# A hybrid network of four layers on one core: convolution by blocks, decays in two parts, output pieces between the scan's steps, and row updates in layer 2

## The chip, the cores and the metric

The kernel is one program on one core of a Trainium2 chip. The core's engines run side by side, each with its own queue of instructions in a fixed order: TensorE (PE, with PEld for its weight loads), VectorE (DVE), ScalarE (ACT), GpSimd (POOL) and SyncE (SP, which here only issues transfers). They wait for each other through semaphores. The metric is the device time of one execution in microseconds (us).

## The reference

The input is x, 4 images of 256 channels by 32x32 places, so 1024 tokens an image and 4096 in all. Everything is float32. What bears on the change is layer 0 (a Mamba-2 block with channel attention) and layer 1:

```python
# layer 0
u = layernorm(tokens(x))                              # eps 1e-5, norm_g, norm_b
z, xBC, dt = split(u @ in_w.T)                        # 256, 512, 4
dt = softplus(dt + dt_bias)
xBC = silu(conv4(xBC) + conv_b)                       # causal, each channel by itself, 4 taps
xs, Bm, Cm = split(xBC)                               # 256 (4 heads of 64), 128, 128
state = state * exp(dt * A) + (dt * x_t) outer B_t    # a scan over the 1024 tokens
y = state @ C_t + Dp * xs
y = y * silu(z);  y = y * rsqrt(mean(y * y) + eps) * rms_w
out = y @ out_w.T
attn = sigmoid(relu(mean_over_tokens(out) @ se1_w.T + se1_b) @ se2_w.T + se2_b)
x = x + out * attn
# layer 1
g, theta, phi = (w @ x + b for each)                  # one number a token
y = theta * sum_over_image(phi * g) / 1024
x = x + (w_w * y - mean) * rsqrt(var + eps) * bn_gamma + bn_beta   # mean, var by channel
```

Layer 2 is attention over each image's 1024 tokens and then a feed-forward layer of 8 experts, of which each token takes two; layer 3 is attention in another form, and an LSTM of 1024 steps.

## The kernel before

A scheduler of the language orders each engine's queue when the kernel is built: instructions go by their place in the program, but one that is ready earlier may move ahead. Only the ends of the attention, the plan of the experts and the LSTM have their order written out by hand. Tiles come from pools with a fixed number of buffers; a new tile waits until an old one is released.

The residual stream lies in SBUF as `rows`, 32 tiles of 128 tokens by 256 channels.

- `_project` walks over 8 blocks of 512 tokens: a block of x is loaded and turned (p_x, L241; ACT copies it to `rows`, L244, and DVE keeps three sums a token for layer 1, of_x, L245), moments by DVE (L133, L134), rstd by POOL (L146, L147), scaling by DVE (L153), turned back (L162, u by ACT, L257), and projected: p_z gives silu(z) (ACT, L273) and dtr (DVE, L274), p_w the 512 channels of xBC (L278, copied by ACT, L281). After every second block `convolve` runs over a whole image of 1024 tokens: for each of 4 groups of 128 channels a scaling by ACT (L288), three taps by DVE (L293), each onto the same `acc`, and a Silu by ACT (L296).
- `_decays` comes once, after all of it: softplus and its products for all 32 tiles in DVE, with Exp and Ln on ACT, and three matmuls (L350) whose Exp gives `head`, `total` and `tail`.
- `_scan` takes an image in 8 steps of 128 tokens: transposes and C by B (ptr, L370, L371), decays within the tile (au by ACT, L381; pd, L383; Exp to m_h, L385; times gm by DVE, L386), products with x (xdt, y, xw by POOL, L389, L395, L398; py, L392), the state's share (pst, L401, L406; DVE, L403, L404, L408, L409), then zs by DVE (L412) and its sum of squares by ACT (L414).
- `_out` does an image's output in one go: rstd by POOL (L426, L427), for each tile a diagonal matrix of rstd by DVE (L434) that PE turns y with (L438; yT by ACT, L442, which also sums up `part`), the channel attention (L447 to L467), the weights times attention (L469), six accumulating products by DVE (L473) for the three columns that layer 1 wants, and eight products (L481), added to `rows` by DVE (L484), with the three columns copied by ACT (L485). The order in the program is scan 0, scan 1, out 0, scan 2, out 1, scan 3, out 2, out 3.
- `_layer1` makes one row and one number a token (L505 to L549), adds bn_beta to `rows` by POOL in 8 pieces (L552) and row times y by DVE in 32 (L554).
- `_layer2_attention` multiplies wq by wk to m_qk (L602 to L612), and its `front` normalises, turns and projects an image. Then scores (p_s, L739), maxima (L744), Exp (L748), transposes (L760) and products (L773) go token tile by token tile.

PSUM has 8 banks: p_x 2, p_z 2 and p_w 4 in the projection; ptr 2, p_o 2, pst 2, pd 1 and py 1 in the scan. The weights of layer 0 come in one load (`w_l0`, 1092 KB, on ACT's queue); `wide` brings five rows of 256 to all partitions.

Of the kernel before, what the change touches and what calls it, by code (L numbers as in the profile page):

```python
# [19 lines left out]
B = 4  # L20
# [51 lines left out]
NW = {"w_l0": 260 + 512 + 256 + 64, "w_l2": 768 + 8, "w_l3": 768, "w_u": 768, "w_v": 768}  # L72
# [92 lines left out]
def _layer0_and_1(s):  # L165

    nc, tc = s.nc, s.tc
    off = DCONV - 1  # L170
    with ExitStack() as ctx:
        keep = ctx.enter_context(tc.tile_pool(name="l0_keep", bufs=1))
        w = keep.tile([P, C, NW["w_l0"]], F32, name="w_l0")
        nc.scalar.dma_start(w, s.d["w_l0"].rearrange("(k p) n -> p k n", p=P))
        se2 = keep.tile([NSE, D], F32, name="se2")
        nc.scalar.dma_start(se2, s.d["w_se2"])
        wide = keep.tile([P, 5, D], F32, name="wide")
        nc.scalar.dma_start(
            wide.rearrange("p i d -> p (i d)"), s.d["wide"].to_broadcast([P, 5 * D])
        )  # L180
        v = SimpleNamespace(
            w_zdt=w[:, :, :ZDT], w_xbc=w[:, :, ZDT : ZDT + 512], w_out=w[:, :, 772:1028],
            w_se1=w[:, :, 1028:1092], se2=se2, se2_b=wide[:, 0, :], beta=wide[:, 1, :],
            three=wide[:, 2:, :],
# [3 lines left out]
            xbc=[keep.tile([P, NXBC, off + L], F32, name=f"xbc{b}") for b in range(B)],  # L188
            zs=[keep.tile([P, TPI, D], F32, name=f"zs{b}") for b in range(B)],
            dtr=keep.tile([P, NT, NH], F32, name="dtr"),  # L190
            ss=keep.tile([P, NT], F32, name="ss"),
        )
        for x in v.xbc:
            nc.gpsimd.memset(x[:, :, :off], 0.0)
        for k in range(C):
            nc.vector.tensor_scalar_mul(
                v.w_out[:, k, :], v.w_out[:, k, :], s.col["rms_w"][:, k : k + 1]
            )
        _project(s, v)
        v.dt, v.decay, v.total, v.tail = _decays(s, keep, v.dtr)  # L200
        with ExitStack() as body:
            pools = SimpleNamespace(
                scan=body.enter_context(tc.tile_pool(name="ssm", bufs=2)),
                out=body.enter_context(tc.tile_pool(name="out", bufs=2)),
                ps=body.enter_context(tc.tile_pool(name="ssm_ps", bufs=2, space=PSUM)),
            )
            for b in range(B):
                _scan(s, v, pools, b)
                if b > 0:
                    _out(s, v, pools, b - 1)  # L210
            _out(s, v, pools, B - 1)
        _layer1(s, v)


def _project(s, v):
# [4 lines left out]
    with ExitStack() as ctx:  # L220
        one = ctx.enter_context(tc.tile_pool(name="proj_one", bufs=1))
        pool = ctx.enter_context(tc.tile_pool(name="proj", bufs=2))
        ps = ctx.enter_context(tc.tile_pool(name="proj_ps", bufs=3, space=PSUM))

        turner = one.tile([P, C, 3 + P], F32, name="turner")
        for k in range(C):
            nc.vector.tensor_copy(turner[:, k, 3:], s.ident)
            for j, name in enumerate(("theta_w", "phi_w", "g_w")):
                nc.vector.tensor_copy(turner[:, k, j : j + 1], s.col[name][:, k : k + 1])
        held = {}  # L230

        def load(i):
# [4 lines left out]
            for j in range(TPB):  # L237
                n = i * TPB + j
                p = ps.tile([P, C, 3 + P], F32, name="p_x", bufs=2)
# [6 lines left out]
            at = slice(i * TPB, (i + 1) * TPB)  # L246
            held[i] = _moments(s, pool, lambda j: s.rows[:, i * TPB + j, :], TPB)
            un = pool.tile([P, TPB, D], F32, name="un")
            _normalise(s, pool, un, s.rows[:, at, :], held[i])
            held[i] = un  # L250
# [12 lines left out]
        def project(i):  # L263
            u = held.pop(i)
            b, t0 = divmod(i * W, L)
            for j in range(TPB):
                n = t0 // P + j
                p = ps.tile([P, ZDT], F32, name="p_z", bufs=2)
# [4 lines left out]
                nc.scalar.activation(v.zs[b][:, n, :], p[:, :D], AF.Silu)  # L273
                nc.vector.tensor_add(v.dtr[:, b * TPI + n, :], p[:, D:], s.row["dt_bias"])  # L274
            for m in range(NXBC):
# [5 lines left out]
                nc.scalar.copy(v.xbc[b][:, m, off + t0 : off + t0 + W], p)  # L281

        def convolve(b):
            for m in range(NXBC):
                x = v.xbc[b][:, m, :]
                acc = pool.tile([P, L], F32, name="acc")
# [5 lines left out]
                for j in range(off):  # L292
                    nc.vector.scalar_tensor_tensor(  # L293
                        acc, x[:, j : j + L], tap[:, j : j + 1], acc, ALU.mult, ALU.add
                    )
# [5 lines left out]
        for i in range(NBLK):  # L301
# [5 lines left out]
            if i % BPI == BPI - 1:  # L307
                convolve(i // BPI)


def _decays(s, keep, dtr):

    nc, tc = s.nc, s.tc
    shape = [P, NT, NH]
    dt = keep.tile(shape, F32, name="dt")
    a = keep.tile(shape, F32, name="a")
    head = keep.tile(shape, F32, name="head")
    total = keep.tile(shape, F32, name="total")  # L320
    tail = keep.tile(shape, F32, name="tail")
    with ExitStack() as ctx:
        pool = ctx.enter_context(tc.tile_pool(name="dec", bufs=1))
        ps = ctx.enter_context(tc.tile_pool(name="dec_ps", bufs=3, space=PSUM))

        e = pool.tile(shape, F32, name="e")
        nc.vector.scalar_tensor_tensor(e, dtr, -1.0, dtr, ALU.mult, ALU.max)
        nc.scalar.activation(e, e, AF.Exp, scale=-1.0)
        e1 = pool.tile(shape, F32, name="e1")
        nc.vector.tensor_scalar_add(e1, e, 1.0)  # L330
        num = pool.tile(shape, F32, name="num")
        nc.scalar.activation(num, e1, AF.Ln)
        none = pool.tile(shape, F32, name="none")
        nc.vector.tensor_single_scalar(none, e1, 1.0, ALU.is_equal)
        nc.vector.tensor_add(num, num, none)
        den = pool.tile(shape, F32, name="den")
        nc.vector.scalar_tensor_tensor(den, e1, -1.0, none, ALU.add, ALU.add)
        nc.vector.reciprocal(den, den)
        nc.vector.tensor_mul(num, num, den)
        nc.vector.tensor_mul(num, num, e)  # L340
        nc.vector.scalar_tensor_tensor(dt, dtr, 0.0, num, ALU.max, ALU.add)

        na = pool.tile([P, NH], F32, name="na")
        nc.scalar.activation(na, s.row["A_log"], AF.Exp)
        nc.vector.scalar_tensor_tensor(a, dt, -1.0, _bc(na, 1, NT), ALU.mult, ALU.mult)

        flat = a.rearrange("p n h -> p (n h)")
        for mat, dst in ((s.upper, head), (s.ones, total), (s.lower, tail)):
            p = ps.tile([P, NT * NH], F32, name="p")
            nc.tensor.matmul(p, mat, flat, start=True, stop=True)  # L350
            nc.scalar.activation(dst.rearrange("p n h -> p (n h)"), p, AF.Exp)
        nc.vector.tensor_mul(tail, tail, dt)
    return dt, (a, head), total, tail


def _scan(s, v, pools, b):


    nc, pool, ps = s.nc, pools.scan, pools.ps
    (a, head), xbc, zs = v.decay, v.xbc[b], v.zs[b]  # L360
    off = DCONV - 1
    state = pool.tile([P, NH, HD], F32, name="state")
    for c in range(TPI):
# [5 lines left out]
        for m in range(3):  # L369
            nc.tensor.transpose(ptr[:, m, :], xbc[:, m, t], s.ident)  # L370
# [1297 lines left out]
```

## Time and profile before

| | us |
|---|---|
| median of 4 runs | 3480.41 (3478.54 to 3484.51) |
| the profiled execution | 3479.1 |
| its span in the profile | 3477.4 |
| PE busy | 3118.7 (90%) |
| DVE busy | 1842.3 (53%) |
| ACT busy | 1091.1 (31%) |
| POOL busy | 535.1 (15%) |
| first pd matmul of the scan (L383) | 152.95 |
| last zs of the scan (L412) | 300.24 |
| layer 1's row ready (L549) | 347.9 |
| first scores of layer 2 (L739) | 384.34 |
| last scores of layer 2 | 690.2 |

The span is the time between the first and the last instruction that the profiler recorded. "Busy" is time in which the engine had an instruction at work; PE's ends are modelled. In the lists of instructions a row has its start, its length, the engine, the line, the operation and tiles, and in brackets how long the engine stood idle before it and what ended that. The chain of waits is followed back from the last instruction: at each step to what released it. Times in the text are from the start of the span.

### The profile page before, as it was taken

Reading aid. Unit: us, or ns where it says so; the run is one execution under the profiler, and the core shown is the slowest. Engines: PE = TensorE matmul, PEld = TensorE weight load, DVE = VectorE, ACT = ScalarE, POOL = GpSimd, SP = SyncE. Lnnn points to the kernel's source line nnn. Section 1 sums busy time; section 2 is a strip of 40 time slices with the busy share of each in tenths; the row PEclk is TensorE's granted clock in tenths of the full one; section 3 lists DMA queues with packets and bytes.
Section 4 is the critical chain, followed back from the end, with each engine's and each line's share of the span. In section 5 each row is a group of like instructions: output and inputs, shape, how many; then the busy total and the mean of one; then the engine's idle time right before and its main releaser. Section 6 shows DMA issues by size and latency. Waiting matters only on the chain.

```text
span 3477.4 us, 143620 instructions
## 1 busy us (share of the span) xinstructions
PE 3118.7 (90%) x63578; PEld 2506.6 (72%) x63578; DVE 1842.3 (53%) x8172; ACT 1091.1 (31%) x4347; POOL 535.1 (15%) x752
## 2 busy tenths in 40 slices
PE   8797899969999979898998998998998998998887
PEld 5465566758888866777777777777777777777776
DVE  5686555541111133565655655655655665665555
ACT  5663222222222222233333332332332332332222
POOL 1153000024444420000100100100100100100000
PEclk9898899979999999999999999999999999999999
DMA  2000000046666630000000000000000000000000
GB/s 81 1 1 19 1 25 26 30 160 191 193 193 192 202 102 1 3 4 4 10 4 4 10 4 4 10 4 4 10 4 4 10 4 4 10 4 6 8 4 10
DMA packets 46003, 135.51 MB, mean 39 GB/s; under 512 B 4864, under 2 KB 34880, under 8 KB 40768
## 3 DMA queue, kind: packets, MB, share of 16 engines
q0 software_dynamic: 19008, 99.32, 9.3%
q1 hardware_dynamic: 24496, 21.27, 1.9%
q8 instruction: 499, 8.18, 1.0%
q10 hardware_dynamic: 1872, 5.68, 0.5%
q14 instruction: 128, 1.05, 0.1%
HBM read 103.95 MB, written 22.32 MB: 36 GB/s over the span
## 4 chain that ended last, share of the span: by engine, by line
PE 54%; DVE 26%; ACT 11%; issue 5%; POOL 1%; DMA 1%; ACTq 0%; DVEq 0%; POOLq 0%; SPq 0%
PE pre L1500 15%; DVE col L1511 11%; PE ph L1111 7%; PE po L1121 7%; PE pre L1462 6%; ACT tri L1514 5%; DVE scan L1523 5%; DVE hs L1534 4%; PE p_a L1420 3%; PE p_d L773 3%; PE p_s L739 3%; DVE acc L293 1%; PE p_o L481 1%; PE p_d L1214 1%; PE p_w L760 1%
## 5 line engine op out<-in xcount | busy, mean ns | idle before, releaser
L1500 PE MATMUL pre<-w_v,hs 128*4 128x64 f32 x49104 | 873.7, 219 | 210.2 <-DVE hs L1534 199.5
L1500 PEld LDWEIGHTS pre<-w_v,hs 128*4 128x4 f32 x49104 | 685.1, 87 | 397.4 <-DVE hs L1534 396.9
L1462 PE MATMUL pre<-xg,pick 128*128 128x64 f32 x6144 | 904.8, 284 | 0.0
L1462 PEld LDWEIGHTS pre<-xg,pick 128*128 128x128 f32 x6144 | 764.5, 191 | 117.8 <-issue 0.8
L1511 DVE STREAM_TRANSPOSE col<-pre 128x64 f32<-128x64 f32 x2048 | 485.0, 250 | 304.1 <-PE pre L1500 286.1
L1514 ACT ACTIVATE tri<-col 128x16 f32<-128x16 f32 x1024 | 229.4, 224 | 1180.8 <-DVE col L1511 1180.8
L1523 DVE TENSOR_TENSOR_SCAN scan<-tri 128x24 f32<-128x24 f32 x1024 | 216.4, 211 | 361.4 <-ACT tri L1514 361.4
L1428 POOL TENSOR_TENSOR xg<-xg,gate_bias 128x192 f32<-128x192 f32 x128 | 75.5, 590 | 1593.0 <-ACT xg L1427 1593.0
L1111 PE MATMUL ph<-xT,wt 128*128 128x256 f32 x1152 | 257.2, 382 | 0.4 <-ACT hT L1114 0.4
L1121 PE MATMUL po<-wt,hT 128*128 128x256 f32 x1152 | 254.6, 379 | 0.0
L1114 ACT ACTIVATE hT<-ph,wt 128x256 f32<-128x256 f32 x288 | 136.2, 473 | 369.6 <-PE ph L1111 369.5
L1111 PEld LDWEIGHTS ph<-xT,wt 128*128 128x128 f32 x1152 | 208.8, 191 | 42.8 <-ACT hT L1114 4.2
L1121 PEld LDWEIGHTS po<-wt,hT 128*128 128x128 f32 x1152 | 216.6, 190 | 27.6
L1532 DVE STREAM_TRANSPOSE gate<-row 128x64 f32<-128x64 f32 x1024 | 227.8, 222 | 0.6
L1521 ACT ACTIVATE row<-pre 128x64 f32<-128x64 f32 x1024 | 209.8, 205 | 0.5
L1539 DVE SCALAR_TENSOR_TENSOR tri<-hs,scan 128x8 f32<-128x8 f32 x1023 | 181.3, 177 | 36.2 <-DVE hs L1534 1.7
L1085 DVE COPY xT<-p_x 128x512 f32<-128x512 f32 x36 | 24.9, 692 | 228.5 <-PE p_x L1081 228.5
L1135 POOL DMA_INDIRECT acc<-y,rows x72 | 114.9, 1596 | 187.7 <-issue 86.7
L1133 DVE TENSOR_TENSOR y<-po,wt 128x256 f32<-128x256 f32 x72 | 30.6, 425 | 204.9 <-PE po L1121 204.9
L1420 PE MATMUL p_a<-w_u,u 128*32 128x192 f32 x1792 | 119.3, 338 | 0.0
L773 PE MATMUL p_d<-v,prT 128*128 128x256 f32 x512 | 117.6, 380 | 0.4 <-DVE v L658 0.4
L739 PE MATMUL p_s<-u,q 128*128 128x512 f32 x256 | 116.3, 596 | 0.0
(2376 smaller groups left out, 3248.1 us busy)
## 6 DMA issues: line engine op xcount, KB each, us to landing
xn<-xn SPq DMA_DIRECT2D x8, 516.0 KB, 3.5
x<-in_x_dram SPq DMA_DIRECT2D x16, 256.0 KB, 3.2
rows<-acc SPq DMA_DIRECT2D x8, 512.0 KB, 7.1
out_dram<-part SPq DMA_DIRECT2D x64, 64.0 KB, 1.7
acc<-rows SPq DMA_DIRECT2D x7, 512.0 KB, 2.9
r<-xn,rows POOLq DMA_INDIRECT x72, 3.3
acc<-y,rows POOLq DMA_INDIRECT x72, 3.9
w_l<-in_w_l_dram ACTq DMA_DIRECT2D x1, 1092.0 KB, 9.8
```

The lines of the kernel that those rows point to most:

```text
L739: nc.tensor.matmul(p[:, h, :], v.q[:, k, bass.ts(j, P)], v.u[:, k, bass.ts(h, W)], start=k == 0, stop=k == C - 1,)
L773: nc.tensor.matmul(p, prT[:, n, :], images[g // TPI].v[:, n, :], start=n == 0, stop=n == TPI - 1)
L1111: nc.tensor.matmul(ph, w1[:, k, bass.ts(m, P)], xT[:, k, :], start=k == 0, stop=k == C - 1)
L1121: nc.tensor.matmul(po, hT[:, m, bass.ts(j, P)], w2[:, m, :], start=m == 0, stop=m == NHC - 1,)
L1420: nc.tensor.matmul(p[32 * j : 32 * (j + 1), :], u3[i * SG // P][:, k, bass.ts(i % (P // SG), 32)], w_u[:, k, j * Q : (j + 1) * Q], start=k ...
L1462: nc.tensor.matmul(p, pick[:, r].rearrange("p j r -> p (j r)"), xg[i][:, v], start=True, stop=t == 0,)
L1500: nc.tensor.matmul(p[32 * j : 32 * j + B, :], hs[:, t - 1, k * B : (k + 1) * B], w_v[:, k, j * Q + v.start : j * Q + v.stop], start=False, ...
L1511: nc.vector.transpose(col[:, g * C : (g + 1) * C, :].rearrange("p n r -> p (n r)"), pre[t % 2][g])
L1514: nc.scalar.activation(z[:, 2:50].rearrange("p (g q) -> p g q", g=2)[:, :, ::3].rearrange("p g (k b) -> p (g k) b", k=C), col[:, :, :B], A ...
L1521: nc.scalar.activation(row, pre[t % 2][2], AF.Tanh)
L1523: nc.vector.tensor_tensor_scan(scan, z[:, 0 : 3 * S], z[:, 26 : 26 + 3 * S], 0.0, ALU.mult, ALU.add)
L1532: nc.vector.transpose(gate.rearrange("p n r -> p (n r)"), row)
```

## The change

It touches layers 0 and 1 and the beginning of layer 2.

- **Convolution by blocks.** `xbc` holds each block of 512 tokens by itself with its own three columns in front; POOL copies a block's last three columns there for the next. Scaling, taps and Silu follow each p_w directly, over 512 tokens.
- **Decays in two parts.** Image 0's eight tiles after block 1, in the middle of the projection; the other 24 after step 1 of the scan.
- **Output pieces among the scan's steps.** `_out` is cut into `_turned` (two tiles), `_attended` and `_product` (one tile). `_scan` keeps a list of pieces and takes two after each step; what is left comes after the last.
- **Channel attention by small products.** The bias of se2 becomes a row of its weights. tanh is taken once as a row and once as a column; the factors 0.5 go into the weights. The three columns come from four matmuls of out_w's transpose with `a3` instead of six DVE products. out_w is transposed at the start (four transposes).
- **Moves.** m_qk (`_keys`) is made ahead of the last image's products, from a w_l2 that is loaded at the projection's end into the place of the input weights. bn_beta is added by POOL to each block of `rows` in the projection. The 32 row updates go into layer 2's `norm`, four before the moments of each block. The load of layer 0's weights is cut in two, with beta's between them.

```diff
-        _project(s, v)
-        v.dt, v.decay, v.total, v.tail = _decays(s, keep, v.dtr)
...
+            nc.scalar.dma_start(w, s.d["w_l0"][:, :NIN].rearrange("(k p) n -> p k n", p=P))
+            nc.scalar.dma_start(v.beta, s.d["bn_beta"].to_broadcast([P, D]))
+            nc.scalar.dma_start(w, s.d["w_l0"][:, NIN:].rearrange("(k p) n -> p k n", p=P))
+            _project(s, v, keep)
+        nc.scalar.dma_start(s.w_l2, s.d["w_l2"].rearrange("(k p) n -> p k n", p=P))
...
+                nc.tensor.transpose(p[:, bass.ts(m, P)], v.w_out[:, m, bass.ts(k, P)], s.ident)
+            nc.scalar.copy(v.w_outT[:, k, :], p[:, :D])
...
+            nc.gpsimd.tensor_add(mine, mine, _bc(v.beta, 1, TPB))
...
-                nc.scalar.copy(v.xbc[b][:, m, off + t0 : off + t0 + W], p)
-        def convolve(b):
-            for m in range(NXBC):
-                x = v.xbc[b][:, m, :]
-                acc = pool.tile([P, L], F32, name="acc")
+                x = v.xbc[b][:, m, half, :]
+                nc.scalar.copy(x[:, off:], p)
+                if half + 1 < BPI:
+                    nc.gpsimd.tensor_copy(v.xbc[b][:, m, half + 1, :off], x[:, W:])
+                acc = v.acc.tile([P, W], F32, name="acc")
...
-            if i % BPI == BPI - 1:
-                convolve(i // BPI)
+            if i == BPI - 1:
+                _decays(s, v, pool, lambda: ps.tile([P, ZDT], F32, name="p_z"), 0, TPI)
...
+def _scan(s, v, pools):
+    aside = []
+    for b in range(B):
+        yT = pools.out.tile([P, C, L], F32, name="yT", bufs=2)
+        part = pools.out.tile([P, C, TPI // 2], F32, name="part", bufs=2)
+        state = pools.scan.tile([P, NH, HD], F32, name="state")
+        for c in range(TPI):
+            _scan_tile(s, v, pools, b, c, state)
+            if b == 0 and c == 1:
+                _decays(s, v, pools.scan, lambda: _small(pools, P, W), TPI, NT)
+            for _ in range(2):
+                if aside:
+                    aside.pop(0)()
+            if c % 2:
+                aside.append(
+                    lambda b=b, c=c, yT=yT, part=part: _turned(s, v, pools, b, c - 1, yT, part)
+                )
+        w = []
+        aside.append(lambda w=w, part=part: w.append(_attended(s, v, pools, part)))
+        if b == B - 1:
+            aside.append(lambda: _keys(s, pools))
+        for c in range(TPI):
+            aside.append(lambda b=b, c=c, yT=yT, w=w: _product(s, v, pools, b, c, yT, w[0]))
+    while aside:
+        aside.pop(0)()
...
+def _turned(s, v, pools, b, c, yT, part):
+    rstd = pool.tile([P, 2], F32, name="rstd", bufs=3)
+    nc.gpsimd.tensor_scalar(rstd, v.ss[:, n : n + 2], 1.0 / D, EPS, ALU.mult, ALU.add)
+    nc.gpsimd.tensor_tensor(rstd, rstd, s.power[:, :2], ALU.pow)
+    for j in range(2):
+        nc.vector.tensor_scalar_mul(diag[:, j, :], s.ident, rstd[:, j : j + 1])
...
-    nc.vector.tensor_add(att, p, v.se2_b)
-    nc.scalar.activation(att, att, AF.Tanh, scale=0.5)
-    nc.vector.tensor_scalar(att, att, 0.5, 0.5, ALU.mult, ALU.add)
+    nc.scalar.activation(att, p, AF.Tanh, scale=0.5)
+            p[:, k : k + 1], v.se2[:, bass.ts(k, P)], hdn[:, 0:1], start=True, stop=True
+    nc.scalar.activation(att_c, p, AF.Tanh, scale=0.5)
...
-            nc.vector.scalar_tensor_tensor(
-                junk, w[:, k, :D], 1.0, v.three[:, j, :], ALU.mult, ALU.mult,
-                accum_out=w[:, k, D + j : D + j + 1],
-            )
+    nc.vector.scalar_tensor_tensor(a3, _bc(att_c, 2, 3), 1.0, v.three, ALU.add, ALU.mult)
+                p[:, bass.ts(m, 3)], v.w_outT[:, k, bass.ts(m, P)], a3[:, k, :],
+    nc.vector.tensor_copy(w[:, :, D:], p.rearrange("p (k j) -> p k j", k=C))
...
-        for i in range(NBLK):
-            mine = s.rows[:, i * TPB : (i + 1) * TPB, :]
-            nc.gpsimd.tensor_add(mine, mine, _bc(v.beta, 1, TPB))
-        for n in range(NT):
-            nc.vector.scalar_tensor_tensor(
-                s.rows[:, n, :], row, y[:, n : n + 1], s.rows[:, n, :], ALU.mult, ALU.add
-            )
...
             def norm(i):
                 n = b * TPI + i * TPB
+                for j in range(n, n + TPB):
+                    nc.vector.scalar_tensor_tensor(
+                        s.rows[:, j, :], s.l1_row, s.l1_y[:, j : j + 1], s.rows[:, j, :],
+                        ALU.mult, ALU.add,
+                    )
...
-    s.wpool = ctx.enter_context(tc.tile_pool(name="weights", bufs=2))
+    s.wpool = ctx.enter_context(tc.tile_pool(name="weights", bufs=1))
```

## The prediction

> **What bounds the kernel now.** I read the busy table and the slices first, then busy time by stage, then the chain of waits up to 420 us, then the timeline of the places that the chain names. In program order one core does layers 0 and 1 (to 348 us), layer 2's attention (to about 720), the experts, layer 3 and the LSTM. After layer 2's first steps the order of every engine is the same in both kernels, so only the first 390 us can change, and what they gain or lose reaches the end, since what follows is a serial chain.
>
> ```profile
> 28.00:130.00 102.00, 95.30 (x367) 58.90 (x365) 68.97 (x153) 70.21 (x119) 6.26 (x10) 1.00 0.04 11
> 130.00:153.00 23.00, 2.79 (x12) 2.53 (x13) 14.73 (x21) 14.39 (x24) 0.00 (x0) 0.58 0.00 0
> 153.00:213.00 60.00, 57.28 (x316) 42.06 (x315) 51.62 (x121) 44.64 (x134) 37.51 (x54) 0.96 0.01 1
> 213.00:300.00 87.00, 78.80 (x461) 61.61 (x460) 74.60 (x189) 47.71 (x156) 43.01 (x53) 1.00 0.00 1
> 300.00:338.00 38.00, 26.82 (x124) 20.18 (x124) 16.77 (x61) 7.92 (x31) 9.20 (x7) 0.82 0.00 0
> 338.00:361.00 23.00, 7.86 (x26) 6.12 (x26) 18.37 (x51) 0.91 (x3) 4.21 (x11) 0.66 0.19 69
> 361.00:384.00 23.00, 18.50 (x63) 11.63 (x64) 15.56 (x57) 3.92 (x6) 5.03 (x8) 0.82 0.00 0
> ```
>
> The columns are the stretch, its length, busy time of PE, PEld, DVE, ACT and POOL, PE's clock, and DMA. PE is full while it projects (28 to 130) and scans (153 to 300). In 130 to 153 it stands nearly idle, and from 300 to 384 it is partly idle. The chain says why:
>
> ```profile
> 134.99 4.88 DVE acc L293 x4
> 139.90 1.30 DVE acc L293
> 142.40 1.28 ACT L344
> 144.12 1.28 ACT L332
> 149.29 1.28 ACT L351
> 153.16 1.71 PE pd L383 x2
> ...
> 307.83 9.35 PE p_o L481 x32
> 328.20 9.38 PE p_o L481 x32
> 347.96 12.76 DVE rows L554 x32
> 384.50 6.87 PE p_s L739 x16
> ```
>
> Between projection and scan stand the last image's convolution and the decays. After the scan stand the output pieces of images 2 and 3, one after the other, layer 1's scalars, 32 row updates, and layer 2's first normalisations.
>
> **From projection to scan.** The mark is the scan's first pd matmul, at 153.16 now. (a) At the start PE has four transposes of w_out behind the first tile's products. They wait for a load that is now third instead of part of the first. The one load lands at 11.57 now and PE resumes at 12.33. Bounds: no delay, and the landing of today's third load of weights, "wide", issued at 6.86 and 7.5 on its way, 14.4, so 2.8 later; I take 1.5. (b) The convolution's 48 taps on DVE (1024 wide) become 96 of 512. Twelve in a row take 14.94, so 1.245 each; half is 0.62, and a 128x512 product (L386) takes 0.69. I take 0.66: 63.4 instead of 59.8. They start with block 0's first p_w (26.3, plus copy 0.58, scaling 0.66 and 1.5) at 29, no longer at 45.4. (c) The eight adds of beta (POOL L552, 2.35 each) now run in the projection. The timeline shows what they do to DVE:
>
> ```profile
> 280.61 2.37 POOL L552 TENSOR_TENSOR rows<-rows,wide 128x1024 f32<-128x1024 f32 x1 [1.58 <-DVE rows L484]
> 281.33 1.93 DVE L408 TENSOR_TENSOR state<-state,total 128x256 f32<-128x256 f32 x1
> ...
> 338.10 2.34 POOL L552 TENSOR_TENSOR rows<-rows,wide 128x1024 f32<-128x1024 f32 x1 [1.35 <-DVE rows L484]
> 338.25 2.31 DVE L505 TENSOR_TENSOR all<-all,of_y 128x96 f32<-128x96 f32 x1 [0.23 <-ACT of_y L485]
> ```
>
> L408 with both inputs in SBUF takes 0.41 elsewhere. It ends only when POOL does, while L484, which reads PSUM, keeps its 0.42 beside the same add. The taps read two SBUF tensors, and in DVE's order taps follow the scaling that each add waits for, from block 2 on: six adds by about 2.1 is 12.6; the bounds are 0 and 14.1.
>
> The Trainium skill (SBUF — State Buffer, "Who interferes with whom") says that a DVE instruction with two SBUF inputs contends with a GpSimd instruction that reads SBUF, the later one waiting in full. No row here shows a tap beside an add; by that rule all six meet, and without it this term is nought and the forecast 12.6 us lower.
>
> (d) DVE from 29 on: taps 63.4, locks 12.6, statistics and scaling of five more blocks (20 tiles by 0.9, from L133, L134, L153, L245 when they follow closely) 18, waits for rstd 5 by 1.24 (L153 idled 9.9 before eight), 30 dtr adds 2.4, the first decays 2: 105, so 134 without other idling. ACT gets six more table loads (1.28 each, 7.7) around the first decays, and DVE is 68% busy here now, so I add 6: 140. PE needs 26 for two blocks (32 passes of L278 by 0.43, 32 of L270 by 0.22, 32 of L241 and 16 of L162 by 0.11) and gets 29.4 today (L288 begins at 44.13, 73.57 and 103.01 in the chain), so it is not the later one. The decays' 9.4 us in series are gone. First pd at 140 instead of 153: 13 gained, between 3 (DVE 88% filled) and 22 (half the locks, no idling). Block-edge copies on POOL are three columns wide, cost under 0.2, and stand behind nothing that DVE waits for.
>
> **The scan.** L412 starts at 160.1 for step 1 and 213.1 for step 16: 3.53 us a step. The next sixteen, with the output pieces of images 0 and 1 in big lumps, take 87.1, so a lump costs (87.1 - 56.5)/2 = 15.3. First pd to last L412 (300.2) is 147. Afterwards three lumps lie inside and three of the four turnings of the last image: 7 + 32 by 3.53 + 3 by 15.3 + 2.9 (three quarters of L438's 3.89) = 169. Off it come: six accumulating products per image with the two passes on att (2.08 + 0.33 + 0.2, less 0.2 for the small ones), 3 by 2.4 = 7; the locks by the adds (L408 at 2.36, 1.91, 1.93 instead of 0.42: 4.9 in two lumps, 7.4 in three); and 3 for spreading. That last is bounded by 0 and by the lump's PE time, 12.5 (32 passes by 0.112, 32 by 0.22, two small products): 8.4 for three. On come 3 for the later decays: three table loads, 3.85, among ACT's work of about 3.0 in a step of 3.53. POOL changes little: 15 pairs of 0.2 + 0.71 (128x2, as L541) in place of three of 1.85 and four adds. Sum 154: 7 lost, between 4 gained and 18 lost. PE's own work in it is 32 by 3.2 (five passes for ptr and eight for py by 0.11, two for pd by 0.43, four for pst by 0.22) plus 3 by 12.5 plus 3, 143, so it fits.
>
> **After the scan.** From last L412 to layer 1's sum being done (340.59) is 40.3. Left are one turning of two tiles (sq 0.6, rstd 0.9, diag 0.4, PE 0.9, ACT 0.9, hand-overs: 5.4), attention 5.6 (6.4 now, from 321.82 to 328.20, less L465 and L467, plus the tiny products), the eight products 9.4 and the copy 0.2. The keys come in here: in PE's order the eight passes of wq by wk and four tiny ones stand ahead of the products and pass two PSUM buffers that ACT empties. Now they run at 348 to 353.6 under the row updates and cost nothing; with that cover gone, 3. The add lock on L505 goes (2.31 to 0.25). Sum 24: 16 gained, between 13 and 19.
>
> **Into layer 2.** From the row at 347.96 to the first scores at 384.34 is 36.4. Four updates (0.4 each) now precede the first statistics, and twelve more stand in DVE's order ahead of the scores. DVE idles 7.4 of the 23 us to 384 and can take some in. The gain is at least 12.8 - 6.4 = 6.4 and at most 12.8 - 1.6 = 11.2; I take 9. The last 16 updates stand around the first score maxima, where DVE waits 39.3 us over the stage for p_s: hidden; without that cover they cost 6.4. The load of w_l3 stands on ACT's queue ahead of layer 2's first copy of u, as it does now ahead of m_qk's; it waits there for DVE and POOL work that the copy comes after anyway. Its issue takes 0.5, and its 5.9 in flight are hidden until 1285 us, its first use. The load of w_l2 moves from 340.6 up to the end of the projection, behind the last product out of w_in, whose place it takes; ACT's last copy of p_w, three entries ahead in its queue, waits for the same product, and its landing (4.3) has the whole scan for cover.
>
> **Sum.** -13 + 7 - 16 - 9 = -31 on a span of 3477.4, in an execution of 3479.1 (1.7 lie around the span), 1.3 under the median of 3480.4. I forecast 3449.
>
> **Rivals.** (A) DVE becomes the bound of the projection: the taps idle as DVE does today, first pd comes at 153 or later. For it: the locks, the rstd waits, the table loads. Against: taps are spread, and 29.4 us per two blocks today holds a burst of 15. Gain 0 + 9 + 16 - 7 = 18 or less; about 3462. (B) The locks mostly miss (the adds fall beside statistics), and the scan goes at PE's rate, 145: 20 + 2 + 17 + 10 = 49; 3431. For it: PE was 95% busy from 153 to 213. Against: ACT and DVE have about 3 us a step as well. (C) Slower: the turnings block PE's queue. Each of the 15 puts four passes behind zs, sq, POOL's rstd pair and diag, 3.0 us of chain; POOL's pair stands in its queue behind later steps' xdt, y and xw (0.61 each), and a PE that waits holds the next step's matmuls. Fully exposed, 45; it decides from 2.1 each (31/15) and would give 3494. Against: in PE's order each turning stands one or two steps after its last zs. (D) The time comes back later, say as waits for the released buffers: 3478. Nothing in the orders speaks for it.
>
> **How the numbers follow.** Forecast 56%, A 20%, B 15%, C 6%, D 3%. The forecast's own bounds (3 to 22, -18 to 4, 13 to 19, 6 to 11) would reach from 4 to 56 if all met at one end; most of it is 15 to 48. The range takes in A and B: 3428 to 3468. About 0.2%, 7 us, is what a measurement can tell from no change. Faster 0.91, within it 0.03, slower 0.06.
>
> **What would show it.** First pd near 140, with taps of 1.9 to 3 us beside POOL's adds; L412's successor 3.5 to 5 us a step and the last near 294; products of the last image in a row of 9.4 followed by layer 1; row updates among the norms and scores some 30 us earlier than 384. Wrong would be: PE idle for several us ahead of the turnings' passes in each step (C), or a first pd past 148 (A), or every stage up to the scores earlier and the end not (D).

## The result, and the profile after

The changed kernel takes 3486.46 us (median of 40 runs, 3483.16 to 3489.28) where the kernel before takes 3480.47 (60 runs beside them): a ratio of 1.0015, 95% interval 1.0010 to 1.0019. That is 5 us slower instead of 31 faster, though still within the 0.2% that I called no change. The profiled execution has a span of 3482.5 us, 5.1 more than before.

Marks in us from the start of the span (where a step begins, if nothing else is said):

| mark | before | after | forecast |
|---|---|---|---|
| first p_w of the projection | 25.3 | 29.4 | 26.8 |
| end of the last p_w | 129.5 | 145.4 | |
| first pd of the scan | 153.0 | 155.5 | 140 |
| from first pd to last zs | 147.3 | 168.8 | 154 |
| from last zs to the end of layer 1's sum | 40.3 | 30.3 | 24 |
| from the row to the first scores | 36.8 | 24.1 | 9 less |
| first scores | 384.3 | 385.3 | 31 less |
| first product of scores and values | 396.4 | 400.8 | 31 less |

So the scan began later instead of earlier, and took 21.5 us longer instead of 7; the 22.7 that the steps behind it gave were used up. Another 3.5 went between the first scores and their first product. From there on the lag stays between 3.7 and 5.1 us to the end. Here are the stages of the changed kernel, in the columns of the table of stages shown before:

```profile
33.00:145.00 112.00, 97.95 (x372) 60.64 (x370) 93.28 (x208) 85.30 (x159) 27.70 (x32) 0.98 0.03 10
145.00:156.00 11.00, 3.64 (x15) 2.49 (x15) 7.32 (x13) 8.36 (x18) 4.41 (x6) 0.73 0.22 74
156.00:213.00 57.00, 52.66 (x294) 40.32 (x293) 43.40 (x112) 40.51 (x127) 27.88 (x46) 0.93 0.00 1
213.00:325.00 112.00, 99.34 (x586) 79.85 (x585) 80.73 (x201) 62.04 (x221) 45.01 (x76) 1.00 0.00 1
325.00:355.00 30.00, 23.24 (x82) 18.89 (x82) 6.30 (x21) 4.25 (x19) 1.52 (x7) 0.62 0.00 1
355.00:362.00 7.00, 2.34 (x10) 1.82 (x10) 3.08 (x15) 0.00 (x0) 1.58 (x9) 0.73 0.34 112
```

In the projection VectorE is now busy for 93 of 112 us and TensorE for 98: two engines near full in one stage, and neither gets there. From 325 to 355 TensorE is busy for 23 of 30 us, VectorE for 6, ScalarE and POOL for less, and TensorE runs at a clock of 0.62 (the granted share of its full speed). The chain of waits of the changed kernel names the work in both places (start, duration, work):

```profile
95.71 4.11 DVE acc L314 x6
...
104.17 4.73 DVE acc L314 x4
...
118.95 2.68 DVE acc L314
...
141.60 0.82 ACT acc L309
142.52 0.76 DVE acc L314
...
150.29 0.80 ACT acc L309
...
330.94 1.85 PE p_o L490 x8
...
336.64 1.87 PE p_o L524 x8
338.50 1.92 PE p_o L549 x4
...
341.31 2.08 PE p_o L549 x4
...
344.29 9.38 PE p_o L537 x32
...
361.60 1.67 DVE rows L675 x4
...
390.23 2.37 DVE rows L675 x6
392.60 1.13 DVE top L799
```

Six undisturbed taps take 4.11, 0.69 each; four take 4.73, and one takes 2.68, where an addition of beta lies beside them. From 141 on, taps and scalings alternate: ScalarE scales a group, VectorE does its three taps, ScalarE the next. At 330 to 344 small products and the keys (L549) stand one behind the other ahead of the last eight products. At 390 six row updates stand ahead of the first maximum (L799).

### The profile page after: what moved, and what is told of

Read it like the earlier page. It is cut to its first block, busy times and chain, and to the rows that moved or that the text cites. A ratio compares the mean times of both kernels' runs of the same rounds, so it can differ in the third digit from the quotient of the medians.

```text
span 3482.5 us, 143921 instructions
## 1 busy us (share of the span) xinstructions
PE 3130.3 (90%) x63636; PEld 2518.9 (72%) x63636; DVE 1844.1 (53%) x8184; ACT 1108.4 (32%) x4428; POOL 548.9 (16%) x792
## 4 chain that ended last, share of the span: by engine, by line
PE 54%; DVE 25%; ACT 12%; issue 6%; POOL 2%; DMA 1%; ACTq 0%; DVEq 0%; SPq 0%; POOLq 0%
PE pre L1555 15%; DVE col L1566 11%; PE ph L1166 7%; PE po L1176 7%; PE pre L1517 6%; ACT tri L1569 5%; DVE scan L1578 5%; DVE hs L1589 4%; PE p_a L1475 3%; PE p_d L828 3%; PE p_s L794 3%; DVE acc L314 2%; PE p_o L537 1%; PE p_d L1269 1%; PE p_w L815 1%
## 5 line engine op out<-in xcount | busy, mean ns | idle before, releaser
L1176 PEld LDWEIGHTS po<-wt,hT 128*128 128x128 f32 x1152 | 216.6, 190 | 27.6
```

Of the source, the lines that this page charges most:

```text
L1176: nc.tensor.matmul(po, hT[:, m, bass.ts(j, P)], w2[:, m, :], start=m == 0, stop=m == NHC - 1,)
```

## The experiments

Each kernel ran beside the kernel before on the same chip; the ratio is to that. Differences "at the end" are differences of ratios times 3480, and the intervals make each of them uncertain by 3.5 to 6.5 us. The LSTM at the end, whose order is the same in all these kernels, took 2072 to 2079 us from its first product (`pre`) on, from profile to profile, so stages are compared at marks of the profile and ends by the ratios.

| run | ratio to before (95%) | first pd | first pd to end of the sum | row to first scores |
|---|---|---|---|---|
| before | 1 | 153.0 | 187.6 | 36.8 |
| after | 1.0015 (1.0010 to 1.0019) | 155.5 | 199.1 | 24.1 |
| e1_no_beta | 0.9982 (0.9973 to 0.9991) | 145.8 | 199.0 | 24.1 |
| e2_conv_image | 1.0001 (0.9992 to 1.0010) | 154.9 | 199.2 | 24.1 |
| e3_lumps | 0.9993 (0.9984 to 1.0002) | 157.7 | 192.0 | 24.1 |
| e4_rows_in_l1 | 1.0037 (1.0023 to 1.0051) | 157.0 | 199.0 | 36.7 |
| e5_keys_early | 1.0007 (0.9998 to 1.0016) | 156.9 | 197.0 | 24.1 |
| e6_early_rstd | 1.0013 (1.0003 to 1.0022) | 158.0 | 198.8 | 24.1 |
| e7_decays_once | 1.0004 (0.9995 to 1.0013) | 152.7 | 201.9 | 24.1 |
| e8_before_rows | 0.9989 (0.9980 to 0.9998) | 152.8 | 193.5 | 26.6 |
| e9_lag | 0.9992 (0.9983 to 1.0001) | 158.5 | 193.4 | 24.1 |
| e10_lumps_beta_pe | 1.0092 (1.0078 to 1.0106) | 147.5 | 233.2 | 27.7 |
| e11_lumps_beta_l1 | 0.9976 (0.9966 to 0.9985) | 145.7 | 193.4 | 27.7 |
| e12_keys_in_l2 | 1.0008 (0.9999 to 1.0017) | 158.2 | 192.8 | 28.2 |
| e13_decays_once | 0.9956 (0.9942 to 0.9969) | 141.8 | 191.8 | 27.6 |
| e14_late_w_out | 0.9954 (0.9940 to 0.9968) | 141.0 | 193.2 | 28.2 |
| e15_conv_image | 0.9981 (0.9972 to 0.9990) | 153.3 | 191.9 | 27.6 |
| e16_late_lag | 0.9983 (0.9974 to 0.9992) | 142.3 | 199.6 | 27.6 |
| e17_columns_by_dve | 0.9963 (0.9949 to 0.9976) | 144.2 | 191.2 | 27.7 |

Seven of them have the same projection in their code (after, e3, e4, e5, e6, e9, e12); their first pd lies between 155.5 and 158.5, mean 157.4.

### The additions in the projection: e1

```diff
-            nc.gpsimd.tensor_add(mine, mine, _bc(v.beta, 1, TPB))
```

> The changed kernel without its eight additions of bn_beta (L272): beta is left out of the output. Theory 1 (the additions hold up the taps): the taps' mean falls from 0.88 to 0.74 us, the first pd matmul moves from 155.5 to 143 to 145, and the end by -10 to -12 (3486 to about 3475). Rival (the additions only fill time in which VectorE would wait for ScalarE's next scaling anyway): first pd at 151 or later, the end -4 or less, and VectorE's idle time ahead of the taps (10.2 us) grows by what the taps lose.

First pd at 145.8 against the mean of 157.4, 11.6 earlier, and the end 11.5 earlier. The group of taps, first of the changed kernel, then of e1 (busy time, mean ns of one, idle time ahead):

```profile
L314 DVE SCALAR_TENSOR_TENSOR acc<-xbc,cols,acc 128x512 f32<-128x512 f32 x88 | 74.8, 883 | 10.2 <-ACT acc L309 9.5
```

```profile
L313 DVE SCALAR_TENSOR_TENSOR acc<-xbc,cols,acc 128x512 f32<-128x512 f32 x89 | 63.6, 748 | 11.4 <-ACT acc L308 10.7
```

The taps lose 11 us of busy time and VectorE's idle time ahead of them grows by 1.2 only, so theory 1 holds. The timeline of the changed kernel shows one such meeting:

```profile
87.90 3.51 DVE L314 SCALAR_TENSOR_TENSOR acc<-xbc,cols,acc 128x512 f32<-128x512 f32 x2
91.40 2.06 DVE L314 SCALAR_TENSOR_TENSOR acc<-xbc,cols,acc 128x512 f32<-128x512 f32 x3
...
88.06 2.80 POOL L272 TENSOR_TENSOR rows<-rows,beta 128x1024 f32<-128x1024 f32 x1 [1.56 <-DVE dtr L296]
```

Two taps take 3.51 us where the three after them take 2.06: POOL's addition begins inside the first tap, and the second ends 0.55 behind it. Six of the eight additions meet a tap in this way.

### The convolution: e2 and e15

```diff
-                acc = v.acc.tile([P, W], F32, name="acc")
+                acc = pool.tile([P, L], F32, name="acc")
...
             project(i)
+            if i % BPI == BPI - 1:
+                convolve(i // BPI)
```

> The changed kernel with the convolution over whole images after every second block, as before; the additions of beta stay in the projection. Theory 2 (the half-size convolution hands work back and forth between ScalarE and VectorE, 10 us of idle VectorE and 14 of idle ScalarE): first pd falls from 155.5 to 146 to 150 and the end by -5 to -9. Rival (spreading the taps is right and only the additions spoil it): first pd at 158 to 166, the end +3 to +10, because the last image's taps again stand in a row at the end.

> e13 with the convolution over whole images. If blocks are a gain once the additions are gone (the last taps, 12 of 1.25 us, no longer behind the last product): first pd 6 to 9 later than e13, at 148 to 153 as before the change, the end +5 to +9. Rival (blocks hand work to and fro between ScalarE and VectorE, 12.7 us of idle VectorE): first pd within 2 of e13 or earlier.

e2 has its first pd 2.5 us ahead of the mean of the seven, between the two theories, and ends 4.9 earlier, at the edge of theory 2. With the additions in place, halving the blocks was a loss. The taps of e2 show why:

```profile
L315 DVE SCALAR_TENSOR_TENSOR acc<-xbc,cols,acc 128x1024 f32<-128x1024 f32 x48 | 59.2, 1280 | 9.8 <-ACT acc L310 9.5
```

They take 1.28 us each, as in the kernel before (1281 ns): none of the eight additions meets one. In blocks six do. e15 has the additions elsewhere, and against it the blocks of e13 (below) are worth 11.5 us of first pd and 8.7 at the end (0.9981 against 0.9956). That pair has the decays once; with the decays in two parts, e1 against e2 says the same: 9.1 earlier and 6.6 at the end. So spreading the taps is right, and the additions had taken it all. Theory 2, that the handing to and fro loses more than it gains, has fallen, for it holds only beside the additions.

### The pieces among the steps: e3, e6, e9, e16

e3 runs all of an image's pieces in one lump behind the next image's steps, as before. e6 writes POOL's rstd pair directly behind its step. e9 writes each turning two steps later. e16 is e14 (below) with e9's pieces.

```diff
 # e3
-            for _ in range(2):
-                if aside:
-                    aside.pop(0)()
...
+        for f in aside:
+            f()
+        aside = now
 # e9
-                if aside:
-                    aside.pop(0)()
+                if aside and aside[0][0] <= b * TPI + c:
+                    aside.pop(0)[1]()
             if c % 2:
-                aside.append(
+                put(b * TPI + c + 2,
```

> The changed kernel with the output of each image in one go at the place it had before, and all else as changed. Theory 3 (the pieces among the steps are what lengthened the scan: VectorE's diagonals wait 11 us for POOL's rstd, TensorE 12 us for the diagonals): from first pd to layer 1's sum 172 to 180 instead of 199 (before: 188), with the last zs 140 to 146 after first pd instead of 169, and the end -15 to -27. Rival (the scan is longer for another reason, the later decays or the products' order): 195 or more, the end within 4 us of the changed kernel's or slower.

> The changed kernel with POOL's rstd pair of each turning (L463, L464) written directly behind its step and no longer one step later with the diagonals. Theory 6 (the diagonals wait because the pair stands in POOL's queue behind the next step's xdt, y and xw): VectorE's idle time ahead of the diagonals falls from 11.1 to under 4 us, first pd to last zs from 169 to 158 to 163, the end -6 to -11. Rival (the pieces' own work fills the engines, and another wait takes the place): 166 or more and the end -3 or less.

> The changed kernel with each turning written two scan steps later than it is (products and attention keep their order behind it). Theory 9 (the diagonals stand in VectorE's queue close behind their own zs, so VectorE holds back the next steps' work until POOL's rstd is there): idle VectorE ahead of the diagonals falls from 12 to under 5 us, first pd to last zs from 169 to 157 to 163, the end -5 to -10. Rival (TensorE's own work, 88% busy at full clock, is the bound, and the waits only fill up what it leaves): 166 or more and the end within 3 us.

> e14 with the output in pieces among the steps, each turning two steps later than in the changed kernel, instead of in one go. If pieces with a lag are as good as lumps: the end within 2 us of e14. If spreading was right and only the wait for rstd spoilt it: the end -3 to -8 against e14. If the pieces cost in themselves: +4 or more.

e3: last zs 141.0 after first pd, as theory 3 said, but 192.0 to the sum and not 172 to 180, for the work that left the scan stood in the tail. The gain is 7.1 us to the sum and 7.7 at the end. Up to the sum the changed kernel had lost 11.5 against the kernel before; the pieces are 7.1 of that.

e6 changed nothing: 11.5 us of idle VectorE ahead of the diagonals, where the waits of the changed kernel have 12.1. The waits of the changed kernel, e6 and e9 (what waited and for what, us in total, times, longest):

```profile
DVE diag L467 <- POOL rstd L464: 12.1, 12, 2.2
DVE diag L474 <- POOL rstd L465: 11.5, 12, 1.7
DVE diag L471 <- POOL rstd L468: 7.1, 7, 2.2
```

Theory 6 has fallen, and the timeline of the changed kernel shows why:

```profile
224.60 0.42 DVE L453 TENSOR_TENSOR zs<-zs,y 128x256 f32<-128x256 f32 x1
226.72 0.63 DVE L467 TENSOR_SCALAR diag<-ident,rstd 128x128 f32<-128x128 f32 x1 [1.69 <-POOL rstd L464]
227.27 0.28 DVE L416 TENSOR_TENSOR gm<-ptr,upper 128x128 f32<-128x128 f32 x1
228.18 0.78 DVE L427 TENSOR_TENSOR m_h<-m_h,gm 128x512 f32<-128x512 f32 x1
...
225.72 0.19 POOL L463 TENSOR_SCALAR rstd<-ss 128x2 f32<-128x2 f32 x1 [10.71 <-ACT sq L455]
225.99 0.69 POOL L464 TENSOR_TENSOR rstd<-rstd,power 128x2 f32<-128x2 f32 x1
```

POOL starts the pair as soon as the sum of squares is there. It is the diagonal that stands too early: the next one in VectorE's queue behind its own zs, it waits out the 1.7 us through ScalarE and POOL, and the next step's gm and m_h wait behind it. e9 puts steps in between: idle time there falls to 7.1 us, first pd to last zs to 163.4, the end by 8. Theory 9 holds, though the idle time stayed above the 5 that it gave.

With this lag the pieces are as good as lumps, and no better: e9 takes 1.4 us more to the sum than e3 and ends with it (0.9992 and 0.9993). In e16 they are worse: against output in one go (e14) 6.4 us more to the sum and 10 more at the end (0.9983 against 0.9954). But e16 has POOL's additions of beta behind the products, so that six of them now lie among the steps, and all six hold up an instruction of VectorE; in e14 four lie there and two do. POOL's xw comes late too. TensorE's waits for it up to the last zs, first in e14, then in e16:

```profile
PE pst L450 <- POOL xw L442: 2.4, 2, 2.1
PE pst L453 <- POOL xw L445: 10.1, 6, 2.8
```

So part of e16's loss lies with the additions, and no run shows that pieces with this lag cost anything in themselves.

### The row updates: e4 and e8

```diff
 # e4 (e8 does the opposite to the kernel before)
         nc.vector.tensor_copy(s.l1_row, p)
+        for n in range(NT):
+            nc.vector.scalar_tensor_tensor(
+                s.rows[:, n, :], s.l1_row, y[:, n : n + 1], s.rows[:, n, :], ALU.mult, ALU.add
+            )
```

> The changed kernel with the 32 row updates back at the end of layer 1. Theory 4 (moving them gains 12 us up to the first scores, and 3.5 of it is given back by the updates that stand around the first maxima): first scores 11 to 13 later, first product of scores and values 7 to 10 later, the end +6 to +9 (3493 to 3496). Rival (hidden anyway): the end within 2 us of the changed kernel's.

> The kernel before with one part of the change alone: the 32 row updates stand in layer 2's norms. Theory 8 (this part is a gain by itself, less what the uncovered products of wq and wk take): from the row to the first scores 26 to 30 instead of 36.8, 3 of it given back around the first maxima, the end -4 to -8 against the kernel before. Rival (the gain needs the other parts or doesn't come through): within 2 us of the kernel before.

e4: from the row to the first scores 36.7 instead of 24.1, and at the first product of scores and values 10.7 later than the changed kernel instead of 14.2 at the first scores: 12.6 gained, 3.5 given back, 7.7 at the end (1.0037 against 1.0015). In e8 the way from row to scores shrank by 10.2 and the end by about 4 (0.7 to 7 by the interval), but its profile has a scan that took 5.1 us longer than in the kernel before, with the same order of instructions. Two stretches of the scan, first e8, then the kernel before:

```profile
213.00:243.00 30.00, 27.08 (x138) 20.27 (x137) 23.57 (x67) 15.95 (x53) 11.47 (x14) 0.89 0.00 1
243.00:273.00 30.00, 27.25 (x148) 20.62 (x146) 21.09 (x52) 14.73 (x48) 13.65 (x19) 0.89 0.00 1
```

```profile
213.00:243.00 30.00, 26.73 (x152) 20.29 (x152) 26.50 (x72) 16.94 (x57) 14.29 (x18) 1.00 0.00 1
243.00:273.00 30.00, 26.19 (x157) 19.90 (x157) 24.61 (x64) 18.38 (x57) 14.89 (x21) 1.00 0.00 1
```

TensorE was granted 0.89 instead of 1.00, once in each of the two lumps. So a single profile of this scan can be 5 us off, and e8's gain is read from the ratio.

### The keys: e5 and e12

```diff
 # e5
-        if b == B - 1:
+        if b == 1:
             aside.append(lambda: _keys(s, pools))
 # e12 drops these two lines, and at the head of layer 2:
+        _keys(s, slim)
```

> The changed kernel with the products of wq and wk (L549, L555) among the scan's steps of image 2 instead of behind the last attention. Theory 5 (at the tail they are uncovered, 5.8 us at half clock where the forecast had 3): from the last zs to layer 1's sum 24 to 25 instead of 30, the scan at most 2 longer, the end -4 to -6. Rival (TensorE is full in the scan, so what leaves the tail comes back there): the end within 2 us of the changed kernel's.

> The changed kernel with the products of wq and wk back at the head of layer 2. Theory 5b (at the tail nothing covers them, at the head of layer 2 the norms do, all but some 2.5 us): last zs to layer 1's sum 24 to 25 instead of 30, row to first scores 25 to 28 instead of 24, the end -2 to -5. Rival (their cost only moves): the end within 1.5 us.

From the last zs to the sum both took 24.8 instead of 30.3. In e5 first pd to last zs grew by 3.4 (172.2 against 168.8), and the end gained 2.8: in the middle between theory and rival. In e12 4.1 came back between row and scores (28.2 against 24.1), and the end gained 2.4. Up to the first scores e12 is 2.2 shorter from first pd than the changed kernel, and e5 2.1 up to the sum. So moving the keys to the tail probably cost between 2 and 3 us: four figures agree, but each is within its uncertainty.

### The decays and the load of w_out: e7, e13, e14

```diff
 # e7, e13
-            if i == BPI - 1:
-                _decays(s, v, pool, lambda: ps.tile([P, ZDT], F32, name="p_z"), 0, TPI)
+            if i == NBLK - 1:
+                _decays(s, v, pool, lambda: ps.tile([P, ZDT], F32, name="p_z"), 0, NT)
 # e14: scaling and turning of w_out in a function
+            if i == 0:
+                weights()
```

> The changed kernel with the decays once, for all 32 tiles, behind the projection. Theory 7 (as forecast: two parts save some 5 us of the chain between projection and scan and cost 3 in the scan): first pd 4 to 8 later, first pd to last zs 2 to 4 shorter, the end +1 to +5. Rival (the later part costs the scan more than it saves): the scan 6 or more shorter, the end -1 or lower.

> The fastest kernel so far (output in one go, additions of bn_beta behind the products, keys in layer 2) with the decays once behind the projection. If two parts only cost the projection ScalarE's table loads (4.7 us in the earlier pair): first pd at 141 to 142 instead of 145.7, and the end -3 to -5 against e11. Rival (without the additions TensorE bounds the projection, 92 to 95% busy, so that ScalarE's loads are hidden, and the serial chain comes behind it): first pd at 146 to 150, the end +1 to +4.

> e13 with the scaling and turning of w_out written behind the first block's projection, so that neither VectorE nor TensorE waits for its load at the start (6 and 5 us). If TensorE bounds the projection: first p_w at 24 to 26 instead of 29, first pd 4 earlier than e13, the end -3 to -5. Rival (ScalarE and VectorE bound it later on): first pd within 1 of e13.

e7 went against my theory and, in the mechanism, against its rival too: with the decays once, first pd came 4.7 earlier than the mean of the seven, and the scan grew by 2.8. At the end 3.8 were gained, just beyond the uncertainty. e13 against e11 confirms it without the additions: first pd 3.9 earlier, the scan 2.1 longer, the end 7.0 earlier. From the end of the last p_w to first pd e7 takes 10.4 and the changed kernel 10.2 (before: 23.5): done once, the decays run among the last block's taps, and the split saved nothing there. e14 moved first p_w by 1 us only; TensorE then waited 4.6 at once for of_x instead, and the end is the same.

### The small products of the attention: e17

```diff
-    a3 = pool.tile([P, C, 3], F32, name="a3")
...
+            nc.vector.scalar_tensor_tensor(
+                junk, w[:, k, :D], 1.0, v.three_b[:, j, :], ALU.mult, ALU.mult,
+                accum_out=w[:, k, D + j : D + j + 1],
+            )
```

> e13 with the three columns for layer 1 by six accumulating products of VectorE, as in the kernel before, and without the small products that replace them (w_out isn't turned at the start; instead three rows are spread over the partitions once, with six diagonals and six products). Theory 10 (the small products stand on the chain at half clock: pooled to first product 7.1 to 7.7 us against 6.4): pooled to first product of the last image about 1 shorter, last zs to layer 1's sum 1 to 2.5 shorter, the start 2 to 4 earlier because nothing waits for w_o there, the end -1 to -5 against e13. Rival (as forecast: the products of VectorE cost 2.4 more in each of the two lumps at the end): last zs to layer 1's sum 3 to 5 longer, the end +2 to +5.

First pd to sum is 191.2 against 191.8, the start is 2.4 later because the three rows are spread there, and the ratios' intervals overlap (0.9963 and 0.9956). In the chain of the last image, from `pooled` to the first product, VectorE's columns take 5.95 (316.67 to 322.62) and the small products 6.75 (314.50 to 321.25). So the small products are no gain; nor are they a loss that the time shows.

### Repairs together: e10, e11 and e13

```diff
 # e10: no additions by POOL, in _product
+    nc.tensor.matmul(p, s.ones[:1, :], v.beta[:1, :], start=False, stop=True)
 # e11: in _layer1, behind the products
+        for i in range(NBLK):
+            mine = s.rows[:, i * TPB : (i + 1) * TPB, :]
+            nc.gpsimd.tensor_add(mine, mine, _bc(v.beta, 1, TPB))
```

> Three repairs of the changed kernel together: output in one go per image at the place it had before; no additions of bn_beta by POOL, instead TensorE adds one pass with a single contraction row per product (32 passes); the products of wq and wk at the head of layer 2 as before. Worked out from the runs so far: -7 (pieces), -9.8 (additions), -3 (keys), +2 to +7 (the passes): first scores at 367 to 374 instead of 385, the end -13 to -18 against the changed kernel, so 7 to 12 faster than before. Rival (the gains overlap, since each only moves a wait): first scores at 378 or later, no faster than before by more than 3.

> As the kernel with three repairs, but the additions of bn_beta by POOL behind each block's products as in the kernel before, and no passes of TensorE for them. -7, -9.8, -3, and +2 to +5 for VectorE's state updates that the additions hold up: first scores at 368 to 372, the end -13 to -17 against the changed kernel. Rival (overlap): 378 or later.

e11 came as worked out, 1.5 late: first scores at 373.5, 13.6 us ahead of the changed kernel at the end. With the decays once, e13 takes 3467.6 us (5 runs) beside 3483.4 of the kernel before, a ratio of 0.9956 (0.9942 to 0.9969): faster than both kernels. Its projection and tail, in the columns of the stages:

```profile
33.00:132.00 99.00, 94.07 (x364) 58.31 (x362) 80.66 (x200) 80.02 (x152) 11.59 (x25) 1.00 0.04 11
132.00:142.00 10.00, 3.96 (x15) 3.43 (x16) 8.33 (x16) 9.20 (x16) 0.00 (x0) 0.59 0.26 81
...
288.00:331.00 43.00, 34.04 (x160) 27.38 (x160) 12.55 (x37) 10.01 (x47) 9.93 (x10) 0.84 0.00 1
```

TensorE is busy for 94 of 99 us of the projection: now it is the bound there. e10 missed by far, 27 us slower than the changed kernel; the section on the hardware shows where.

## Why the prediction was wrong

**Projection to scan, 13 earlier (came: 2.6 later, 4.4 by the mean of the seven).** (a) The start cost 4.1 instead of 1.5: first p_w at 29.4. (b) The taps were priced a little low: in e1, without additions, the 96 are 69.2 us of busy time, 0.72 each, against 0.66 and 63.4. (c) The locks were right in mechanism and nearly in size: six additions met taps, and they cost 11.6 against 12.6. The failed step is (d). It says that TensorE, with 26 for two blocks, "is not the later one". I held the 26 against the 29.4 that the projection gets today, when it should have been held against my own sum for VectorE: four times 26 is 104, and VectorE's sum was 105. TensorE already ran at that rate: in the kernel before, the last p_w ends 104.2 after the first begins, and my table of stages had it busy for 95 of 102. Two engines with equal work that hand each other blocks did not take the longer of the two here: from first p_w to the end of the last it was 116. Even without the locks (e1) the last p_w ends at 135.6, close to 29.4 + 104, and what my sum had no term for stands behind it: the last block's four groups going between ScalarE and VectorE, 8.6 to the last tap at 144.2, and 1.5 to first pd. The locks come on top. "The decays' 9.4 us in series are gone" was right, but not by the split: e7 has them once and they are gone too, while the first part costs the projection some 4 us (e7, e13).

**The scan, 7 longer (came: 21.5).** The figures of a step and of a lump hold within some 5 us: the same terms for a scan with two lumps and no pieces (7 + 113 + 2 by 15.3, less 4.8 for small products and 4.9 for locks, plus 3) give 143.9, and e3 took 141.0. Two of the small terms were not there: e17 shows no gain by the small products, and without the later decays the scan was longer, not 3 shorter (e7, e13). What failed is the subtraction of 17 for a scan with pieces. The 3 for spreading was a cost instead: the pieces are 7.1 of the way to the sum (e3), and the lag of e9 alone gives 5.7 of it back. That is rival C's chain at a third of its price, about 1 us of idle VectorE at each of 12 diagonals in place of 3.0 at each of 15. I gave C 6%, because in TensorE's order each turning stands one or two steps behind its last zs; I had not looked at VectorE's order, where the diagonal stands next behind it. Nor was the 7 for the small products there (e17).

**After the scan, 16 less (came: 10.0).** The products took the 9.4 that I gave them. The turning took 6.2 instead of 5.4, the attention 7.6 instead of 5.6 (to 338.50), and the keys 5.8 instead of 3. I had taken TensorE's passes at full clock in a stretch that was granted 0.62.

**Into layer 2, 9 less (came: 12.7, above my bound of 11.2).** Then the last updates, which I called hidden, cost 3.5 of the 6.4 that I named for a lost cover: six of them stand ahead of the first maximum. The net is 9.2. That it is the figure that I had is luck, two misses that cancel; e4 shows the gain and the loss.

Rival A (first pd at 153 or later) met the mark of the projection, though not its cause: A has VectorE alone as the bound, and without the additions TensorE is (94 of 99 us in e13). C had the chain of the scan, and TensorE did wait for the diagonals (11.6 us in 10 places), but C did not see that VectorE's queue is held as well. I had worked out each with all other terms as forecast. Both came together, and that case I had not given a time.

## What to carry to other kernels

When a stage has two engines near full, add each one's work over the whole stage from the new sums and compare those; if they are within a few per cent, add the fill at the end and the waits of one for the other instead of taking the longer. For a step that is spread among others, look at the order of every engine that it passes, above all at what stands behind an instruction whose input still has to go through two other engines. Work put into a stretch where the profile shows a low clock is paid at that clock, and an elementwise addition on POOL is free only beside VectorE instructions that the trace shows undisturbed.

## What the runs showed of the hardware

Products with a single contraction row were not cheap at all. In e10 each of 32 products has one more such pass (two instructions in the profile). In the last image, from the groups (busy, mean ns) and the stages of e10:

```profile
L536 PE MATMUL p_o<-w_att,yT 128*128 128x259 f32 x32 | 16.7, 678 | 0.4 <-DVE w_att L527 0.4
L537 PE MATMUL p_o<-beta,ones 1*128 1x259 f32 x17 | 10.4, 710 | 0.0
```

```profile
300.00:350.00 50.00, 43.68 (x135) 29.29 (x135) 8.28 (x30) 8.47 (x38) 3.37 (x8) 0.59 0.00 1
350.00:395.00 45.00, 37.06 (x88) 23.22 (x86) 11.20 (x40) 2.60 (x12) 1.87 (x10) 0.50 0.06 18
```

An instruction with one row takes as long as one with 128 (710 ns beside 678). And TensorE, though busy for 37 of 45 us, was granted 0.50 all along, where the same products without these passes bring the clock back up within the stretch (0.84 over the tail in e13; in e11, the closest to e10, 0.54 from 320 to 330 and 0.93 from 330 to 337). From first pd to the sum e10 takes 233.2 us and e11 193.4. The Trainium skill (TensorE: Matmul & The Clock Gate, "The HAM clock gate") says that the gate follows how busy TensorE has been. By the profile's busy time it was as busy here (82% of the stretch) as over the tail in e13 (79%), so that busy time alone does not tell the clock. e10 and e11 also differ in POOL's additions, and why products of one row would keep the clock low was not tried any further.
